# Causal mask of the first attention blocks: from GpSimd, after the exponential, to VectorE, before it

## The chip, the cores and the metric

The kernel runs on one core of a Trainium2 chip. The metric is the time on the device in microseconds (us) for one execution of the whole program. A profile of one execution gives, for each engine, when each instruction started, how long it was busy and what it waited for.

## What is computed

The reference is a small model of two layers on 2 x 2048 tokens of width 256. The first layer adds causal self-attention with 16 heads of width 16 and a feed-forward part with eight experts, of which a router picks two for each token; the second adds a state-space (Mamba) part and a ternary projection. The change lies in the attention, cut to what matters here:

```python
scores = jnp.einsum('bhqd,bhkd->bhqk', q, k) * scale
causal = jnp.tril(jnp.ones((s, s), dtype=bool))
scores = jnp.where(causal[None, None, :, :], scores, -jnp.inf)
weights = jax.nn.softmax(scores, axis=-1)
attn = jnp.einsum('bhqk,bhkd->bhqd', weights, v)
```

The router (`top_k` over eight logits) decides to which expert's rows each token is copied.

## The kernel before

The program is a chain of parts: layer norms and projections (to about 184 us), attention together with the router, the experts (from 1285 us), and the state-space part (from about 1925 us). Tile, the layer under the kernel, orders each engine's instructions when the program is built; on the chip every engine then runs its own list in that order and waits on semaphores.

Attention works on 16 stages, one for each pair of heads of each batch element (`stages()`). A stage has two passes over the causal half of the score matrix, in chunks of `CH` = 512 queries, `NJ` = 4 of them:

- `maxima(s)`: PE computes scores `m` of 128 queries by up to 512 keys for both heads (L652). On the diagonal block VectorE adds a mask (L662, 0 or a large negative number) in PSUM. VectorE then takes the row maxima into `best` (L665). When a chunk is done, its negated maxima are turned into rows, `tops` (L668 to L687).
- `attend(s)`: PE computes the scores transposed, 128 keys (`kb`) by 512 queries, into `s`, and adds the negated maxima with a second pair of matmuls (both L750). ScalarE (ACT) writes the exponential to `p` in SBUF (L758). Where the key block lies on the diagonal (`kb >= QT * j`, 4 of them in a chunk, 16 in a stage, 256 in all), GpSimd (POOL) sets the upper triangle of `p` to zero with an affine select (L763). PE multiplies `p` by the values (`values`, L705, tile `pv`).

The two passes run interleaved: in each tick a generator for `attend` and one for `maxima` advance by one block, `attend` 22 ticks (`LAG`) behind. Both passes draw their score tiles from one PSUM pool of three buffers (tag `sc`). The products of a block are issued one to two ticks after its exponential (`due`, `now`). The q and k of a stage are loaded on SyncE's queue (L554) from DRAM into a pool of three buffers, one stage ahead.

The router's work is spread between these ticks: every third step of the loop advances the generator `routing` by one. After some vector work in the first stages it loads 32 blocks of 128 rows on SyncE's queue (L973), and for each issues two indirect scatters on GpSimd (L984, tile `x_d`, 64 in all) that copy the rows to their experts' places. All scatters write the one DRAM tile `x_d`, so each waits for the one before. `routing` ends when the scatters are issued; the loop goes on with attention alone.

Of the kernel before, what the change touches and what calls it, by code (L numbers as in the profile page):

```python
# [11 lines left out]
F32 = mybir.dt.float32  # L12
F32R = mybir.dt.float32r
AF = mybir.ActivationFunctionType
ALU = mybir.AluOpType
# [4 lines left out]
P = 128  # L20
# [24 lines left out]
BIG = 3.0e38  # L45
# [56 lines left out]
def tile_model(ctx: ExitStack, tc: tile.TileContext, t, out):  # L102
# [55 lines left out]
    with ExitStack() as c0:  # L158
# [9 lines left out]
        with tc.tile_pool(name="vs", bufs=1) as vsp, tc.tile_pool(name="qk", bufs=3) as qk:  # L168
# [6 lines left out]
            with tc.tile_pool(name="pa", bufs=2) as pa, tc.tile_pool(  # L175
# [144 lines left out]

            routes = []
            attention(
                tc,
                t,
# [215 lines left out]
def stages():  # L540

    return [(b, pr) for b in range(B) for pr in range(H // 2)]
# [19 lines left out]
def attention(tc, t, ident, ones, qk, qk_d, stacks, v, xa, router):  # L562
# [6 lines left out]
    nc = tc.nc  # L569
    NJ = S // CH  # L570
    QT = CH // P
# [3 lines left out]
    with ExitStack() as ctx:  # L575
        w = ctx.enter_context(tc.tile_pool(name="at_w", bufs=1))
# [10 lines left out]
        for g in range(NG):  # L587
# [9 lines left out]
            out=mask,  # L597
            in_=mask,
            pattern=[[-1, P]],
            compare_op=ALU.is_ge,  # L600
            fill=-BIG / 10,
            base=0,
            channel_multiplier=1,
        )
        zeros = w.tile([P, P], BF, name="zeros")
        nc.gpsimd.memset(zeros, 0.0)

# [86 lines left out]
        def attend(s, attn):  # L694

            b, pr = stages()[s]
            qT, kT = stacks[s]

            def values(j, kb, off, pt):
                for h in range(2):  # L700
                    for f in range(2):
                        lo, hi = max(off, f * HC), (f + 1) * HC
                        if lo < hi:
                            r0 = 32 * (2 * h + f)
                            nc.tensor.matmul(  # L705
                                pv[r0 : r0 + HS + 1, lo - f * HC : HC],
                                lhsT=v[:, b * TPB + kb, 2 * pr + h, :],
                                rhs=pt[:, h, lo:hi],
                                start=(kb == 0),
                                stop=(kb == (QT * j + 1 if f == 0 else QT * j + 3)),  # L710
                                tile_position=(0, r0),
                            )

            def finish(j, raw):
                u = f"{s}_{j}"
                tr = ps_m.tile([P, 2, 2, 2, 32], F32, tag="misc", name=f"tr_{u}")
                for k in range(2):
                    nc.tensor.transpose(
                        tr[:, k].rearrange("p h f i -> p (h f i)"), raw[:, k * P : (k + 1) * P], ident
                    )  # L720
                inv = sm.tile([P, 2, 2, 2], F32, tag="inv", name=f"inv_{u}")
                nc.vector.reciprocal(inv, tr[:, :, :, :, HS])
                for f in range(2):
                    c0 = 2 * pr * HS
                    nc.vector.tensor_tensor(
                        attn[j][:, 2 * f : 2 * f + 2, c0 : c0 + 2 * HS].rearrange("p k (h i) -> p k h i", i=HS),
                        tr[:, :, :, f, 0:HS],
                        inv[:, :, :, f].unsqueeze(3).to_broadcast([P, 2, 2, HS]),
                        ALU.mult,
                    )  # L730
                if pr == H // 2 - 1:
                    done.append(output(b, j, attn[j]))

            def leave(j):
                raw = sm.tile([P, HC], F32, tag="raw", name=f"raw_{s}_{j}")
                nc.scalar.copy(raw, pv)
                turns.append(lambda: finish(j, raw))

            for j in range(NJ):
                if pr == 0:  # L740
                    attn[j] = vp.tile([P, QT, D], F32, tag="attn", bufs=4, name=f"attn_{b}_{j}")
                tp = tops.pop((s, j))
                for kb in range(QT * (j + 1)):
                    off = max(0, kb - QT * j) * P
                    ps = ps_s.tile([P, 2, CH], F32, tag="sc", name=f"s_{s}_{j}_{kb}")
                    pt = pp.tile([P, 2, CH], F32, tag="pt", name=f"p_{s}_{j}_{kb}")
                    for i in range(2):
                        for h in range(2):
                            hs = slice(HP * h, HP * (h + 1))
                            nc.tensor.matmul(  # L750
                                ps[:, h, off:CH],
                                lhsT=(kT[hs, kb * P : (kb + 1) * P], onesr[hs, :])[i],
                                rhs=(qT[hs, j * CH + off : (j + 1) * CH], tp[hs, off:CH])[i],
                                start=(i == 0),
                                stop=(i == 1),
                                tile_position=(HP * h, 0),
                            )
                    nc.scalar.activation(  # L758
                        pt[:, :, off:CH], ps[:, :, off:CH], AF.Exp, scale=float(HS) ** -0.5
                    )  # L760
                    if kb >= QT * j:
                        dg = pt[:, :, off : off + P]
                        nc.gpsimd.affine_select(  # L763
                            out=dg,
                            in_=dg,
                            pattern=[[0, 2], [1, P]],
                            compare_op=ALU.is_ge,
                            fill=0.0,
                            base=0,
                            channel_multiplier=-1,  # L770
                        )
                    due.append(lambda a=(j, kb, off, pt): values(*a))
                    if kb == QT * (j + 1) - 1:
                        due.append(lambda j=j: leave(j))
                    yield

        def output(b, j, attn):

            aT = sm.tile([P, 2, CH], F32, tag="aT", bufs=1, name=f"aT_{b}_{j}")
            for k in range(2):  # L780
                ps = ps_m.tile([P, CH], F32, tag="misc", name=f"aTp_{b}_{j}_{k}")
                for i in range(QT):
                    nc.tensor.transpose(
                        ps[:, i * P : (i + 1) * P], attn[:, i, k * P : (k + 1) * P], ident
                    )
                nc.scalar.copy(aT[:, k, :], ps)
                yield
            for c in range(2):
                po = ps_m.tile([P, 2, D], F32, tag="misc", name=f"po_{b}_{j}_{c}")
                for i in range(2):  # L790
                    at = (2 * c + i) * P
                    for k in range(2):
                        nc.tensor.matmul(
                            po[:, i, :],
                            lhsT=aT[:, k, at : at + P],
                            rhs=wo[:, k, :],
                            start=(k == 0),
                            stop=(k == 1),
                        )
                n0 = b * TPB + j * QT + 2 * c  # L800
                nc.vector.tensor_tensor(xa[:, n0 : n0 + 2, :], xa[:, n0 : n0 + 2, :], po, ALU.add)
                yield
# [10 lines left out]
        def second():  # L813
            for s in range(n_stages):
                yield from attend(s, attn)

        routing = router(rt, ps_m)
# [4 lines left out]
        for at, x in enumerate(tiles):  # L822
            if at % 3 == 0:
                now = due[:]
                del due[:]
                turn = turns.pop(0) if turns else None
            next(x, None)
            if at % 3 == 2:
                for f in now:
                    f()  # L830
                if turn:
                    turn()
                elif done and next(done[0], done) is done:
                    done.pop(0)
                next(routing, None)
        for x in (one, two):
            for _ in x:
                pass
# [1128 lines left out]
```

## Time and profile before

| | |
|---|---|
| median of 3 runs | 3077.14 us (3073.25 to 3079.84) |
| profiled execution, its own time | 3080.93 us |
| its span, first to last instruction | 3079.2 us |
| mean granted TensorE clock | 0.897 of full |
| PE busy | 2634.9 us (86%) |
| DVE (VectorE) busy | 2043.7 us (66%) |
| ACT (ScalarE) busy | 1592.4 us (52%) |
| POOL (GpSimd) busy | 1187.6 us (39%) |
| L763, the select on GpSimd | 256 times, 103.3 us busy |
| L984, the scatters on GpSimd | 64 times, median 972 ns each |

In the profile PE is the matrix engine and PEld its weight loads, DVE is VectorE, ACT ScalarE, POOL GpSimd, SP SyncE. A row of the waits reads: the engine and line that waited, the engine and line that it waited for, the sum in us, the number of waits and the longest. A row of the windows reads: the stretch, its length, and for each engine its busy time and number of instructions, then the clock that TensorE was granted as a share of full speed, and the share of time in which the DMA engines were busy. A row of the groups has the line, engine, operation, the tile written and read, the shapes and count; behind the bar stand the busy time in us, the mean of one in ns, and the idle time ahead of it with what ended that. A row of the timeline has the start, the duration, the instruction, and in brackets the idle time ahead of it.

### The profile page before, as it was taken

How to read it: one execution, taken by the hardware profiler on the slowest of the kernel's cores; microseconds unless marked ns; L12 is line 12 of the kernel's file. 1: busy time of each engine (PE TensorE's matmuls, PEld its weight loads, DVE VectorE, ACT ScalarE, POOL GpSimd, SP SyncE). 2: the span in 40 equal slices, each digit the busy share in tenths (PEclk: the TensorE clock that was granted, in tenths of full speed). 3: DMA queues.
4: the chain of work that ended last, by engine and by line, in shares of the span. 5: the costliest groups of instructions: out<-in, count | busy, mean ns of one | idle time of the engine just before them, and what ended most of it. 6: DMA issues, size and time to landing. Idle time of an engine off the chain costs nothing. (4 is left out here: it accounts for less than half of the span.)

```text
span 3079.2 us, 39986 instructions
## 1 busy us (share of the span) xinstructions
PE 2634.9 (86%) x15021; PEld 1493.3 (48%) x15021; DVE 2043.7 (66%) x2558; ACT 1592.4 (52%) x2546; POOL 1187.6 (39%) x934
## 2 busy tenths in 40 slices
PE   6887888999999999799999999577778888788747
PEld 4543433445444444488888888333333343333303
DVE  6576766888788888324111011258999999999996
ACT  3424555666566666422222222456766676666643
POOL 4313223010111011111111111247887978878775
PEclk9978988999999999899999999677887888879758
DMA  8843214112232220434345553323544535445350
GB/s 290 214 133 80 57 51 86 29 29 42 50 48 29 29 29 1 151 134 144 133 150 194 183 193 109 77 54 85 120 111 104 131 78 133 110 102 117 82 116 14
DMA packets 120614, 309.58 MB, mean 101 GB/s; under 512 B 28464, under 2 KB 70832, under 8 KB 102880
## 3 DMA queue, kind: packets, MB, share of 16 engines
q1 hardware_dynamic: 100496, 206.57, 28.3%
q0 software_dynamic: 18576, 99.24, 9.6%
q8 instruction: 122, 2.00, 0.3%
q10 hardware_dynamic: 1344, 1.16, 0.1%
q14 instruction: 76, 0.62, 0.1%
HBM read 228.51 MB, written 78.38 MB: 100 GB/s over the span
## 5 line engine op out<-in xcount | busy, mean ns | idle before, releaser
L758 ACT ACTIVATE p<-s 128x1024 f32<-128x1024 f32 (+3 forms) x640 | 563.2, 900 | 382.4 <-PE s L750 361.5
L665 DVE TENSOR_REDUCE best<-m 128x2 f32<-128x1024 f32 (+3 forms) x640 | 669.6, 1062 | 111.6 <-PE m L652 101.0
L1855 POOL TENSOR_TENSOR hh<-hh,cc 128x2048 f32<-128x2048 f32 x128 | 579.9, 4531 | 10.3
L1843 DVE TENSOR_TENSOR_SCAN hh<-decay,uh 128x2048 f32<-128x2048 f32 x128 | 565.9, 4421 | 23.8 <-ACT decay L1729 10.1
L705 PE MATMUL pv<-p,v 128*17 128x256 f32 (+1 forms) x4608 | 383.8, 379 | 49.0 <-POOL p L763 46.1
L763 POOL TENSOR_SCALAR_AFFINE_SELECT p<-p 128x256 f32<-128x256 f32 x256 | 103.3, 408 | 785.6 <-ACT p L758 784.5
L1729 ACT ACTIVATE decay<-dd,a_neg 128x511 f32<-128x511 f32 x512 | 332.9, 712 | 53.4 <-DVE hh L1843 52.8
L1118 ACT ACTIVATE hT<-h,b1s 128x256 f32<-128x256 f32 x296 | 137.7, 473 | 384.3 <-PE h L1111 384.3
L1132 DVE TENSOR_TENSOR yt<-o,b 128x512 f32<-128x512 f32 x37 | 25.6, 692 | 436.9 <-PE o L1124 436.9
L1753 DVE TENSOR_TENSOR uh<-dd,bb 128x2048 f32<-128x2048 f32 x128 | 293.6, 2294 | 21.5 <-PE bb L1740 11.6
L750 PE MATMUL s<-q,k 64*128 64x512 f32 (+3 forms) x1280 | 288.2, 437 | 22.9 <-DVE best L665 17.6
L652 PE MATMUL m<-k,q 64*128 64x512 f32 (+3 forms) x1280 | 281.6, 426 | 17.6 <-DVE best L665 8.9
L1111 PE MATMUL h<-xT,w 128*128 128x256 f32 x1184 | 276.1, 387 | 19.7 <-ACT hT L1118 8.1
L1124 PE MATMUL o<-w,hT 128*128 128x256 f32 x1184 | 262.7, 380 | 0.0
L1074 POOL DMA_INDIRECT w<-in_w,wrow x74 | 71.1, 961 | 479.2 <-PE h L1111 255.5
L1111 PEld LDWEIGHTS h<-xT,w 128*128 128x128 f32 x1184 | 226.7, 193 | 54.8 <-ACT hT L1118 8.5
L750 PE MATMUL s<-tops,onesr 64*128 64x512 f32 (+3 forms) x1280 | 248.5, 371 | 0.0
L1124 PEld LDWEIGHTS o<-w,hT 128*128 128x128 f32 x1184 | 225.7, 191 | 30.9
L1770 PE MATMUL y<-hh,sel 128*32 128x512 f32 x1024 | 162.1, 710 | 78.8 <-POOL hh L1855 78.6
L705 PEld LDWEIGHTS pv<-p,v 128*17 128x17 f32 x4608 | 107.9, 97 | 232.4 <-issue 113.5
L750 PEld LDWEIGHTS s<-q,k 64*128 64x128 f32 x1280 | 127.0, 188 | 168.1 <-DVE best L665 56.6
L652 PEld LDWEIGHTS m<-k,q 64*128 64x128 f32 x1280 | 129.3, 192 | 131.7 <-ACT p L758 68.1
(341 smaller groups left out, 3477.2 us busy)
## 6 DMA issues: line engine op xcount, KB each, us to landing
dd<-dd_d SPq DMA_DIRECT2D x120, 512.0 KB, 7.1
q<-qk_d SPq DMA_DIRECT2D x128, 128.0 KB, 5.1
k<-qk_d SPq DMA_DIRECT2D x128, 128.0 KB, 7.5
x_d<-zero SPq DMA_DIRECT2D x6, 1664.0 KB
xg<-x_d SPq DMA_DIRECT2D x37, 256.0 KB, 6.6
y_d<-yt SPq DMA_DIRECT2D x37, 256.0 KB
qk_d<-qp SPq DMA_DIRECT2D x16, 512.0 KB, 7.3
qk_d<-kp SPq DMA_DIRECT2D x16, 512.0 KB, 4.0
```

The source lines that it names most:

```text
L652: nc.tensor.matmul(ps[:, h, 0:n], lhsT=qT[hs, qs], rhs=kT[hs, c * CH : c * CH + n], start=True, stop=True, tile_position=(HP * h, 0),)
L665: nc.vector.tensor_reduce(best[:, i, :, c], ps[:, :, 0:n], AX.X, ALU.max)
L705: nc.tensor.matmul(pv[r0 : r0 + HS + 1, lo - f * HC : HC], lhsT=v[:, b * TPB + kb, 2 * pr + h, :], rhs=pt[:, h, lo:hi], start=(kb == 0), s ...
L750: nc.tensor.matmul(ps[:, h, off:CH], lhsT=(kT[hs, kb * P : (kb + 1) * P], onesr[hs, :])[i], rhs=(qT[hs, j * CH + off : (j + 1) * CH], tp[h ...
L758: nc.scalar.activation(pt[:, :, off:CH], ps[:, :, off:CH], AF.Exp, scale=float(HS) ** -0.5)
L1111: nc.tensor.matmul(ph, lhsT=w1[:, k * DF + f * P : k * DF + (f + 1) * P], rhs=xT[:, k, :], start=(k == 0), stop=(k == 1),)
L1124: nc.tensor.matmul(po[:, h, :], lhsT=hT[:, f, h * P : (h + 1) * P], rhs=w2[:, f * D : (f + 1) * D], start=(f == 0), stop=(f == NF - 1),)
L1729: nc.scalar.activation(decay[G % 2][:, q, 1:], of[at]["dd", n // 4][:, 0, q, 1:], AF.Exp, scale=a_neg[:, q, n : n + 1],)
L1753: nc.vector.tensor_tensor(uh, of[at]["dd", n // 4][:, 1], of[at]["bb", n].to_broadcast(full), ALU.mult)
L1770: nc.tensor.matmul(of[at]["y"][C4 * q : C4 * (q + 1), :], lhsT=sel, rhs=hh[:, q, :], start=False, stop=(g == 3), tile_position=(0, C4 * q),)
L1843: nc.vector.tensor_tensor_scan(hh.rearrange("p q c -> p (q c)"), decay[G % 2].rearrange("p q c -> p (q c)"), uh.rearrange("p q c -> p (q c)"),
L1855: nc.gpsimd.tensor_tensor(hh, hh, m_["cc", g].to_broadcast(full), ALU.mult)
```

## The change

A second mask, `mask_t`, is built once on GpSimd: 0 where the query is not before the key, a large negative number elsewhere. A list, `routed`, is empty until the generator `routing` has ended. While it is empty, the diagonal blocks of `attend` get `mask_t` added in PSUM by VectorE before the exponential, which makes the masked weights zero. From then on the select on GpSimd follows the exponential as before. In the program as built, the first 72 of the 256 diagonal blocks take the new way, and 184 the old.

```diff
+        mask_t = w.tile([P, P], F32, name="mask_t")
+        nc.gpsimd.memset(mask_t, 0.0)
+        nc.gpsimd.affine_select(
+            out=mask_t,
+            in_=mask_t,
+            pattern=[[1, P]],
+            compare_op=ALU.is_ge,
+            fill=-BIG / 10,
+            base=0,
+            channel_multiplier=-1,
+        )
+        routed = []
...
+                    if kb >= QT * j and not routed:
+                        dg = ps[:, :, off : off + P]
+                        nc.vector.tensor_tensor(
+                            dg, dg, mask_t.unsqueeze(1).to_broadcast([P, 2, P]), ALU.add
+                        )
                     nc.scalar.activation(
                         pt[:, :, off:CH], ps[:, :, off:CH], AF.Exp, scale=float(HS) ** -0.5
                     )
-                    if kb >= QT * j:
+                    if kb >= QT * j and routed:
                         dg = pt[:, :, off : off + P]
                         nc.gpsimd.affine_select(
...
-                next(routing, None)
+                if next(routing, routed) is routed:
+                    routed.append(True)
```

## The prediction

> **What bounds the kernel now.** I read the slices of the page first, to find the stretch that the change touches.
>
> ```profile
> PE   6887888999999999799999999577778888788747
> DVE  6576766888788888324111011258999999999996
> POOL 4313223010111011111111111247887978878775
> PEclk9978988999999999899999999677887888879758
> ```
>
> A slice is 77 us. Attention runs from 184 to 1285 us, slices 3 to 17. In its first five slices PE is at 7 or 8 tenths with a granted clock below full; after that it is at 9. The chain that ended last starts at 1944 us, in the state-space part, so it says nothing here, but attention ends before anything behind it starts, so what it loses the span loses. Next the windows. I cut attention where `attend` begins a new head pair (the first exponential, L758, of each group of 40), so that every row holds the same work: the matmul count, 538 to 546, shows it.
>
> ```profile
> core 0: us, PE busy (x) PEld busy (x) DVE busy (x) ACT busy (x) POOL busy (x), PEclk, DMA share, GB/s
> 209.90:289.70 79.80, 69.23 (x542) 32.18 (x544) 59.30 (x122) 40.79 (x61) 23.09 (x33) 0.85 0.16 49
> 289.70:360.80 71.10, 60.02 (x538) 28.55 (x536) 51.85 (x84) 40.08 (x60) 16.49 (x27) 0.90 0.26 54
> 360.80:437.30 76.50, 62.34 (x542) 28.46 (x538) 51.29 (x85) 40.14 (x61) 18.66 (x28) 0.91 0.27 59
> 437.30:510.80 73.50, 63.67 (x546) 29.59 (x544) 52.26 (x85) 39.93 (x60) 22.98 (x33) 0.91 0.33 78
> 510.80:584.20 73.40, 60.85 (x538) 28.78 (x538) 52.32 (x85) 40.09 (x61) 13.65 (x24) 0.88 0.25 47
> 584.20:646.30 62.10, 59.36 (x542) 27.54 (x538) 51.17 (x85) 39.98 (x61) 6.46 (x16) 1.00 0.24 34
> 646.30:707.00 60.70, 58.80 (x546) 28.12 (x544) 52.09 (x85) 39.75 (x60) 6.45 (x16) 1.00 0.26 38
> ```
>
> The first five stages take 79.8 + 71.1 + 76.5 + 73.5 + 73.4 = 374.3 us. Eight later ones, leaving out the two that also project the first batch element, take 59.5 to 62.2, mean 61.0, with PE busy 58.6, DVE 51.7 and ACT 39.9. Five such stages would be 305: the first five lose 69 us. PE itself splits the loss: it is idle 58.2 us in them against 12.1 in five later ones (46 more), and busy 316.1 against 292.8 (23 more, the same matmuls at a lower clock). Then who was waited for, from 209.9 to 584.2 us:
>
> ```profile
> POOL p L763 <- ACT p L758: 166.2, 41, 26.2
> POOL x_d L984 <- DMA x_d<-rows,slots: 127.0, 55, 7.9
> PEld pv L705 <- POOL p L763: 55.8, 29, 11.3
> PE pv L705 <- POOL p L763: 45.6, 15, 11.0
> ```
>
> PE waits 45.6 us, in 15 pieces, for masks on GpSimd, and that is the 46 of extra idle. GpSimd itself waits 127 us for its scatters to land. The timeline shows one case whole:
>
> ```profile
> 529.26 0.39 PE L750 MATMUL s<-q,k 64*128 64x256 f32 x2 [0.18 <-DVE best L665]
> ...
> 533.54 0.97 POOL L984 DMA_INDIRECT x_d<-rows,slots  x1 [7.66 <-DMA x_d<-rows,slots]
> 536.28 0.97 POOL L984 DMA_INDIRECT x_d<-rows,slots  x1 [1.77 <-DMA x_d<-rows,slots]
> 537.27 1.12 POOL L763 TENSOR_SCALAR_AFFINE_SELECT p<-p 128x256 f32<-128x256 f32 x3
> 537.74 0.15 PEld L705 LDWEIGHTS pv<-p,v 128*17 128x17 f32 x8 [8.18 <-POOL p L763]
> 537.74 1.06 PE L705 MATMUL pv<-p,v 128*17 128x256 f32 x8 [7.97 <-POOL p L763]
> ```
>
> A scatter waits until the one before it has landed, 2.7 us from issue to issue, and up to 8.6 when the load of the next q and k is in flight. Masks of 0.41 us stand behind it in GpSimd's order, and PE, whose order is fixed too, stops at the first product that needs one.
>
> **The change, part by part.** In the built order 72 masks (16 in each of the first four stages, 8 in the fifth) leave GpSimd and become an add on VectorE between the score matmuls and the exponential. On GpSimd all 64 scatters now stand ahead of the remaining 184 masks.
>
> *Setup.* One more memset and select on GpSimd: 0.29 + 0.29 us by the same pair at 183 us. GpSimd then rests until 211 us, so nothing; without that cover 0.6 us.
>
> *Removed.* Of the 69 us I leave 7.6 where they are: the first stage has DVE at 59.3 against 51.7, and this is the router's own vector work, which stays. The rest, 62 us, I give to the scatters, idle time and lowered clock alike: -62. The clock part is the less certain, and PE's 45.6 us of idle alone is the lower bound. The Trainium skill ("TensorE: Matmul & The Clock Gate", Part 1 and "HAM oscillation") has an idle window of about 3.4 us halve the clock and prices the lowered time at half of it. The windows give 1 - PEclk times length, summed over the five, as 41 us, so by that rule the loss would be 46 + 41 = 87 us where the rows give 69: part of the lowered time fell where PE was idle anyway, so the rows decide.
>
> *Added.* VectorE gets 72 adds of 128x256 f32 in PSUM plus a broadcast mask, which is exactly the form that L662 runs already:
>
> ```profile
> L665 DVE TENSOR_REDUCE best<-m 128x2 f32<-128x1024 f32 x114 | 137.5, 1221 | 15.5 <-PE m L652 14.0
> L662 DVE TENSOR_TENSOR m<-m,mask 128x256 f32<-128x256 f32 x64 | 27.5, 429 | 12.4 <-PE m L652 9.7 <-ACT p L758 2.0 <-issue 0.6
> ```
>
> 72 x 0.429 = 30.9 us, or 6.9 in a full stage. Does DVE's idle time cover it? A stage has 61.0 - 51.7 = 9.3 us of it, which would be enough, but not where the adds come. They come four in a row, one to a diagonal block, and in those runs (5.1 to 7.4 us long in the later stages) DVE has 0.1 to 1.3 us idle, about 0.6, and PE less. Perfect packing leaves 1.72 - 0.6 = 1.1 us of a run, 19 us for 18 runs. Nothing absorbs semaphore gaps, so I take the full price, 31 us.
>
> *The wait that is added.* VectorE's add waits for PE's score matmuls. Behind it on VectorE stand the next row-maximum reductions; the exponential waits for it on ACT, and PE waits for that exponential, because the next `m` tile takes the buffer that it frees (three are shared). How long an add sits behind a reduction the trace of before cannot show. From below: the hop through GpSimd between exponential and product goes, worth 8.2 us in 28 waits from 560 to 1200 us, 0.05 us a mask, -3.5 us in all. From above: every add waits out a whole 1.22 us reduction, 72 x 1.22 = 88 us. In the built order the add stands nearly always ahead of the reduction of the same tick, as PE produces them; 8 of 72 stand ahead of a reduction whose tile PE finishes first. I take zero, nearest the row of L662, which waited 12.4 us in 64 cases for its matmuls, DVE being early rather than late.
>
> *Queues.* Scatters no longer stand behind masks. The row loads on SyncE wait for scatters as before, and the q and k loads behind them have more than a stage of lead. SyncE also holds back rows until a q buffer is free, once a stage. So the last row comes as the fifth stage starts, and its two scatters end some 12 us later (two of 2.7 and one slow landing); the first mask left on GpSimd is the fifth stage's ninth, about 30 us in. Nothing is added; if it fails, one stall like those of before, 8 to 11 us.
>
> *Sum.* -62 + 31 = -31 us. By stage: 61 + 7.6 + 6.9 = 75.5, three of 67.9, one of 64.4: 343.6 against 374.3. The profiled execution took 3080.9 us (span 3079.2), 3.8 above the median of 3077.1; -31 gives 3050 for it and 3046 for the median.
>
> **Rivals.**
>
> *Slack hides the adds.* DVE's 9.3 us a stage is taken up after all, PE running ahead by its buffers. For: 6.9 is below 9.3. Against: the runs above have no such room. Cost 0 to 15 us, time 3015 to 3030, say 3022 (cost 7).
>
> *VectorE's queue becomes the bound, and it is slower.* On average an add finds a reduction half done: 0.43 + 0.61 = 1.04 us on the path for each mask, 75 us, so 62 saved and 75 paid: +13, 3090. It decides from 62 / 72 = 0.86 us a mask. For: DVE would be at 58.6 of 61.0 us, 96%, and exponential, buffer and next matmul form a loop through it. Against: PE feeds both in DVE's order. The Trainium skill ("Perfetto Trace Analysis", Optimizing Scalar/DVE Operations) says to move work off a saturated DVE, to GPSIMD if need be, the opposite of this edit; the 85% that DVE shows in the later stages says that it isn't saturated yet.
>
> *The scatters still reach the path.* Unhindered they run into the fifth stage, or the slow clock stays for another reason: idle comes back by one or two stalls and half of the 16 us of clock (62 - 46): 3046 + 18 = 3064.
>
> **How the numbers follow.** The forecast has 0.60 (cost 19 to 45 us, so 3034 to 3060), slack 0.13, queue 0.13, scatters 0.14. A measurement of this kernel can tell about 0.2%, 6 us. Slower by that is the queue case, with a little of it that only breaks even: 0.12. Within 6 us: 0.06, from its edge and the worst of the scatter case. Faster: 0.82. The range goes from slack at its likely price, 3022, to 3072, where the last of the gain is still there; left out are most of the queue case and the bottom of the slack case.
>
> **What would show it.** Right: a VectorE row of 72 adds near 429 ns; L763 at 184; PE's wait for GpSimd at L705 under 5 us from 45.6; PEclk 1.00 from the second stage on; stages of 64 to 68 us with DVE at 58 to 59; scatters 2.7 us apart, without masks between. Wrong: the stages stay over 72 with PE now waiting for ACT at L652 or for DVE at L750 (queue), fall to 62 (slack), or GpSimd's first mask comes right behind a scatter with PE waiting (scatters). If the clock stays below 1.00 without stalls, my giving all 16 us of it to the scatters was wrong.

## The result and the profile after

The changed kernel takes 3027.8 us (median of 4 runs, 3027.2 to 3030.9) against 3075.2 us for the kernel before beside it (3073.1 to 3079.8): a ratio of 0.985, 95% interval 0.983 to 0.986, or 47 us less. The forecast was 31 us less, 3046, with a range from 3022 to 3072. The direction, the place and the removed stall came as forecast; the price of the added work was put at about twice what it is. The profiled execution took 3027.2 us, with a span of 3025.5.

The slices of the page of the changed kernel (76 us each; attention is in slices 3 to 17):

```profile
PE   6879999999999999799999997677878788887846
DVE  6569888887888886232110101368999999999996
POOL 4302221110001101111112111268897887978875
PEclk9969999999999999899999998787887878889758
```

PE is at 9 tenths from the fourth slice on, where before it stayed at 7 and 8 through the seventh. Then the windows of the changed kernel, cut by the same rule, at the first exponential of a head pair:

```profile
core 0: us, PE busy (x) PEld busy (x) DVE busy (x) ACT busy (x) POOL busy (x), PEclk, DMA share, GB/s
210.80:283.30 72.50, 67.77 (x546) 30.79 (x544) 62.59 (x136) 41.37 (x62) 14.00 (x14) 0.89 0.11 35
283.30:346.60 63.30, 59.50 (x544) 27.94 (x540) 56.54 (x101) 40.10 (x62) 15.45 (x16) 1.00 0.41 91
346.60:412.30 65.70, 61.24 (x544) 27.50 (x540) 56.30 (x101) 40.52 (x61) 13.52 (x14) 1.00 0.38 77
412.30:477.70 65.40, 61.45 (x544) 28.36 (x540) 56.60 (x101) 40.30 (x61) 17.38 (x18) 1.00 0.39 87
477.70:537.90 60.20, 56.55 (x532) 27.00 (x530) 52.98 (x91) 39.49 (x60) 5.18 (x10) 1.00 0.25 38
```

The five stages sum to 327.1 us, 47.2 less than the 374.3 of before. The clock is full from the second on, and the later stages agree with those of before within 0.4 us (62.2 against 62.1, 61.0 against 60.7 and so on). So the whole gain lies in these five. (In the two profiled executions the span differs by 53.7; of that 8.1 us lie behind attention, where the work is the same. In the profiles below, that part took between 1796 and 1806 us; I therefore compare stages rather than spans wherever a few us matter.)

The waits of the changed kernel, 210.8 to 537.9 us:

```profile
POOL x_d L1003 <- DMA x_d<-rows,slots: 135.7, 59, 8.1
ACT p L776 <- DVE s L773: 57.9, 55, 7.0
PEld m L665 <- ACT p L776: 41.4, 83, 1.2
PEld pv L718 <- POOL p L781: 0.4, 1, 0.4
```

The lines have moved: L1003 is the scatter, L773 the new add, L776 the exponential, L781 the select, L718 the product with the values. GpSimd waits for its scatters as long as ever, but nothing waits for it any more. PE's wait for GpSimd has gone from 55.8 us in 29 waits (the weight loads of `pv`) to 0.4 in one, and no wait of PE's own matmuls on it is left. A smaller one has come: the exponential now waits for VectorE, 57.9 us in 55 waits, and PE's load for the next `m` waits for the exponential twice as often (41.4 us in 83 waits; 20.0 in 49 before).

VectorE's groups, 283.3 to 537.9 us, hold the new row:

```profile
L675 DVE TENSOR_TENSOR m<-m,mask 128x256 f32<-128x256 f32 x64 | 27.4, 429 | 9.7 <-PE m L665 8.0 <-issue 0.4 <-ACT tops L700 0.4
L773 DVE TENSOR_TENSOR s<-s,mask_t 128x256 f32<-128x256 f32 x55 | 23.3, 424 | 1.6 <-PE s L763 0.9 <-PE m L665 0.6
```

### The profile page after: what moved, and what is told of

The parts are those of the page before. It is cut to its first block, busy times and chain, and to the rows that moved or that the text cites. A ratio compares the mean times of both kernels' runs of the same rounds, so it can differ in the third digit from the quotient of the medians.

```text
span 3025.5 us, 39961 instructions
## 1 busy us (share of the span) xinstructions
PE 2616.7 (86%) x15021; PEld 1484.5 (49%) x15021; DVE 2063.7 (68%) x2630; ACT 1592.7 (53%) x2546; POOL 1159.4 (38%) x864
## 5 line engine op out<-in xcount | busy, mean ns | idle before, releaser
L776 ACT ACTIVATE p<-s 128x1024 f32<-128x1024 f32 (+3 forms) x640 | 564.3, 900 | 337.9 <-PE s L763 256.3
L678 DVE TENSOR_REDUCE best<-m 128x2 f32<-128x1024 f32 (+3 forms) x640 | 670.7, 1063 | 68.4 <-PE m L665 58.6
L718 PE MATMUL pv<-p,v 128*17 128x256 f32 (+1 forms) x4608 | 377.6, 373 | 4.3 <-ACT raw L749 3.8
L781 POOL TENSOR_SCALAR_AFFINE_SELECT p<-p 128x256 f32<-128x256 f32 x184 | 74.4, 406 | 664.6 <-ACT p L776 663.9
L1789 PE MATMUL y<-hh,sel 128*32 128x512 f32 x1024 | 163.7, 716 | 76.8 <-POOL hh L1874 76.6
L718 PEld LDWEIGHTS pv<-p,v 128*17 128x17 f32 x4608 | 106.8, 96 | 181.5 <-issue 114.0
```

The source lines that it names most:

```text
L678: nc.vector.tensor_reduce(best[:, i, :, c], ps[:, :, 0:n], AX.X, ALU.max)
L718: nc.tensor.matmul(pv[r0 : r0 + HS + 1, lo - f * HC : HC], lhsT=v[:, b * TPB + kb, 2 * pr + h, :], rhs=pt[:, h, lo:hi], start=(kb == 0), s ...
L776: nc.scalar.activation(pt[:, :, off:CH], ps[:, :, off:CH], AF.Exp, scale=float(HS) ** -0.5)
L1789: nc.tensor.matmul(of[at]["y"][C4 * q : C4 * (q + 1), :], lhsT=sel, rhs=hh[:, q, :], start=False, stop=(g == 3), tile_position=(0, C4 * q),)
```

## The experiments

Three questions were open: is the stall that went wholly the scatters' doing, what do the adds cost by themselves, and why. Stages in us, cut as above, first to fifth:

| kernel | 1 | 2 | 3 | 4 | 5 | sum |
|---|---|---|---|---|---|---|
| before | 79.8 | 71.1 | 76.5 | 73.5 | 73.4 | 374.3 |
| changed | 72.5 | 63.3 | 65.7 | 65.4 | 60.2 | 327.1 |
| before, no scatters | 68.8 | 59.5 | 62.2 | 60.6 | 59.6 | 310.7 |
| changed, no scatters | 72.8 | 63.1 | 65.8 | 65.4 | 60.3 | 327.2 |
| changed, product after the exponential | 66.6 | 61.4 | 63.9 | 61.8 | 60.7 | 314.4 |
| changed, each add twice | 76.8 | 74.6 | 74.8 | 72.6 | 65.4 | 364.2 |
| changed, again | 69.0 | 63.1 | 65.8 | 65.4 | 60.3 | 323.6 |

### The kernel before without its scatters

```diff
-            nc.gpsimd.indirect_dma_start(
-                out=x_d[:, :],
-                out_offset=bass.IndirectOffsetOnAxis(ap=slots[:, i, n : n + 1], axis=0),
-                in_=rows,
-                in_offset=None,
-            )
```

> The kernel before, with the 64 scatters left out (the experts then work on empty rows; the masks stay on GpSimd). Theory A, masks stand behind scatters on GpSimd and PE waits for them: the five slow stages go to 61 us, the first to about 69 with the router's vector work, so 62 us less than before, 3013, and PE's wait for GpSimd at the value products falls from 45.6 us to under 2. Rival B, the slow clock and the idle time have another cause (the router's vector work, the loads of q and k): the stages stay over 70 and the time within 15 us of before.

Measured: 3012.9 us (3010.9 to 3014.1), ratio to before 0.979 (0.978 to 0.981), 61.5 us less than the 3074.4 beside it. Its windows:

```profile
210.80:279.60 68.80, 64.76 (x540) 30.23 (x540) 59.00 (x122) 40.61 (x62) 6.75 (x16) 0.92 0.21 59
279.60:339.10 59.50, 56.83 (x538) 27.31 (x538) 51.84 (x85) 39.86 (x60) 6.50 (x16) 1.00 0.25 35
339.10:401.30 62.20, 59.48 (x542) 27.62 (x538) 51.30 (x85) 40.06 (x61) 6.45 (x16) 1.00 0.27 36
401.30:461.90 60.60, 58.70 (x546) 28.15 (x544) 51.99 (x85) 39.84 (x60) 6.50 (x16) 1.00 0.27 37
461.90:521.50 59.60, 56.92 (x538) 27.23 (x538) 51.90 (x85) 39.87 (x60) 6.50 (x16) 1.00 0.26 36
```

With the router's vector work (DVE 59.0 in the first stage) and the q and k loads still there and the scatters gone, stages two to five are undisturbed ones and the clock is full in them. Rival B falls: idle time and lowered clock were both the scatters'. One thing more moves in this run: with no scatter to wait for, the 32 row loads on SyncE are all issued by 262.5 us, where before they ran until 519.6. They aren't the cause, since in the changed kernel they run until 475.2 without a stall. PE's own wait for GpSimd at the products, 45.6 us before, is gone, as expected (under 2); the weight loads' wait there is down from 55.8 us to 4.0 in 14 waits of at most 0.4, the ordinary hop from select to product.

The first stage keeps 7.8 us over 61.0, but its row says something else than the prediction did. PE is busy 64.8 us in it, against 58.6 in an undisturbed stage, and idle only 1.6 us more. The granted clock is 0.50 in the stage's first 10.8 us and full after them, 0.92 over the whole stage. PE is busy for 10.0 us of these 10.8, so as an estimate the half clock is worth up to 5 of the 7.8 us. Most of it, then, is a low clock at the start of attention, and not PE waiting for the router's vector work; no run here leaves that work out.

### The changed kernel without its scatters

The same lines are taken out of the changed kernel.

> The changed kernel, with the 64 scatters left out (the experts work on empty rows). Theory A, the scatters are wholly off the path once no mask stands behind them: the same as the changed kernel, 3028, and about 15 us above the kernel before without scatters, which is the price of the 72 adds (0.2 us each, not the 0.43 that I took). Rival D, the scatters still cost something beside the masks (traffic, row loads in front of the q and k loads): well below, 3013 to 3020, and the adds cost nearly nothing.

Measured: 3023.8 us (3023.1 to 3035.9), ratio 0.983 (0.981 to 0.985). The median lies 2 to 4 us under the two medians of the changed kernel, less than the part behind attention varies, so the stages decide: 327.2 against 327.1, and each of the five within 0.3 us. Rival D falls. Once no mask stands behind them, the scatters cost nothing, whether by their traffic or by the row loads on SyncE, which here too are all issued early (by 265.3 us). And the 72 adds cost 327.1 - 310.7 = 16.4 us, 0.23 each. Stages two to five alone, with 56 adds, give 254.6 - 241.9 = 12.7, again 0.23. By the medians the price comes out at 11 to 15 us; so 16 is its upper end.

### All 256 masks added by VectorE

```diff
-                    if kb >= QT * j and not routed:
+                    if kb >= QT * j:
...
-                    if kb >= QT * j and routed:
+                    if False:
```

> The changed kernel with all 256 masks added by VectorE, none left on GpSimd. It measures the price of 16 adds in a stage where nothing else is going on. By the stages of the changed kernel (2 to 5 us a stage over 61, say 4): 11.5 more stages, 46 us, 3074. By the price on record, 6.9 us a stage: 79 us, 3107. If the adds are free and the extra of the changed kernel's stages comes from the scatters: 3028.

Measured: 3067.4 us (10 runs, 3064.1 to 3072.5), ratio 0.998 (0.997 to 0.999): nearly all of the gain is spent. Against the kernel without scatters, four undisturbed stages (the eleventh to the fourteenth) take 63.1, 65.5, 65.7 and 63.4 us where that has 59.6, 62.1, 60.7 and 59.7: 3.9 us for 16 adds, 0.24 each. So the price is the same with the router and without it. My 3074 was 7 us too high, and 3107, by the price of the prediction, 40.

### The mask after the exponential

```diff
-                    if kb >= QT * j and not routed:
-                        dg = ps[:, :, off : off + P]
-                        nc.vector.tensor_tensor(
-                            dg, dg, mask_t.unsqueeze(1).to_broadcast([P, 2, P]), ALU.add
-                        )
                     nc.scalar.activation(
                         pt[:, :, off:CH], ps[:, :, off:CH], AF.Exp, scale=float(HS) ** -0.5
                     )
+                    if kb >= QT * j and not routed:
+                        dg = pt[:, :, off : off + P]
+                        nc.vector.tensor_tensor(
+                            dg, dg, mask_t.unsqueeze(1).to_broadcast([P, 2, P]), ALU.mult
+                        )
```

`mask_t` then holds 1 and 0.

> The changed kernel with the first 72 masks still on VectorE, but as a product with a 0/1 mask in SBUF after the exponential, so that the exponential and the PSUM buffer no longer wait for VectorE. If what the adds cost is VectorE's time: 3028 again, with a few us for a shorter or longer instruction. If it is the later exponential and with it the later release of the PSUM buffer: most of the 15 us goes, 3014 to 3018, and PE's wait at L665 for ACT falls back.

Measured: 3012.6 us (3010.8 to 3013.3), ratio 0.980 (0.978 to 0.981): as fast as with no scatters at all, and faster than both kernels. The product is as long as the add (median 416 ns against 423) and VectorE as busy (55.8 us in the second stage against 56.5), but PE's load for `m` waits for the exponential only 17.8 us in 45 waits, down from 41.4 in 83:

```profile
PEld m L665 <- ACT p L771: 17.8, 45, 0.9
```

This speaks for the second reading: the add's cost came mostly from its place. The run changes two things at once, though: the product stands behind the exponential, and it works in SBUF and no longer in PSUM.

### Each add twice

```diff
-                        nc.vector.tensor_tensor(
-                            dg, dg, mask_t.unsqueeze(1).to_broadcast([P, 2, P]), ALU.add
-                        )
+                        for _ in range(2):
+                            nc.vector.tensor_tensor(
+                                dg, dg, mask_t.unsqueeze(1).to_broadcast([P, 2, P]), ALU.add
+                            )
```

> The changed kernel with each of the 72 adds done twice (72 more of 0.42 us on VectorE, all ahead of their exponentials). If the low price of the first add (16 us for 72, 0.23 each) comes from idle time of VectorE that it fills, the second finds less of it and costs nearer to its full 0.42: 26 to 31 us, 3054 to 3059. If the price is only a fixed delay of waiting in VectorE's queue, paid once, the second adds its own length less than wholly: 10 to 16 us, 3038 to 3044.

Measured: 3070.1 us (9 runs, 3063.9 to 3075.9), ratio 0.997 (0.996 to 0.999). The second add costs 364.2 - 327.1 = 37 us, 0.52 each (41 us against the second profile of the changed kernel): more than either reading gave, and more than its length. It isn't that VectorE had no idle time left:

```profile
292.00:366.60 74.60, 65.89 (x541) 29.72 (x539) 62.32 (x117) 40.24 (x60) 19.45 (x20) 0.89 0.39 91
366.60:441.40 74.80, 67.03 (x544) 29.42 (x542) 62.36 (x117) 40.62 (x61) 12.64 (x13) 0.91 0.32 62
```

VectorE rests 12 us in each of these, and the clock has fallen again, so the first reading, that the second add finds no idle time to fill, falls as well. The timeline of this kernel shows what happens:

```profile
306.70 1.22 DVE L678 TENSOR_REDUCE best<-m 128x2 f32<-128x1024 f32 x1
307.83 0.42 DVE L774 TENSOR_TENSOR s<-s,mask_t 128x256 f32<-128x256 f32 x1
308.17 1.22 DVE L678 TENSOR_REDUCE best<-m 128x2 f32<-128x1024 f32 x1
309.30 0.75 DVE L774 TENSOR_TENSOR s<-s,mask_t 128x256 f32<-128x256 f32 x2
```

The scheduler set a 1.22 us reduction between the two adds of one block, and the exponential stands behind all of it (L774 is the add here); taking VectorE's adds in pairs, such a reduction stands in 35 of the 72. So this run lengthened the delay and not only the work, and it doesn't price an add by itself. Nor are its 37 us all delay: PE is idle 20 us longer than in the changed kernel and busy 17 us longer, with a clock of 0.89 to 0.95. How much each part is worth this run doesn't separate.

### All masks after the exponential

The kernel with the product, with the two conditions changed as for all 256 adds.

> All 256 masks as a product on VectorE in SBUF after the exponential, none on GpSimd. Beside the run with all 256 adds ahead of the exponential (3067) it prices the same work at the other place. Theory C, the add costs mostly because exponential and buffer release wait for it: the products cost the 0.7 us a stage that they cost in the first five stages, 3013 + 8 = 3021. If VectorE's time is what counts: the same 4 us a stage as the adds, 3067 less the router's stages, some 3055.

Measured: 3029.1 us (3027.4 to 3034.0), ratio 0.984 (0.983 to 0.986), where the same masks ahead of the exponential gave 3067. The four stages compared above take 61.4, 63.9, 61.7 and 61.7 us: 1.65 us over the kernel without scatters, against 3.9 for the adds. The 8 us that I expected rested on 0.7 us a stage, a mean over five that the first stage had spoiled: in it the product kernel was 2.2 us faster than the one without scatters, and in the next three it was 1.2 to 1.9 us slower, 1.6 in the mean, which agrees with the 1.65. PE's waits for the exponential, four stages each; ahead of it (all 256 adds, 878.2 to 1135.8 us), then behind it (all 256 products, 853.8 to 1102.5 us):

```profile
PEld m L665 <- ACT p L776: 37.2, 72, 1.2
PE m L665 <- ACT p L776: 9.8, 25, 0.8
```

```profile
PEld m L665 <- ACT p L771: 15.7, 39, 0.9
PE m L665 <- ACT p L771: 1.2, 5, 0.4
```

With the select on GpSimd the first of these rows has 18.9 us in 47 waits in four undisturbed stages of the changed kernel.

### The changed kernel again

> The changed kernel once more, beside the others on this chip: 3028, the first five stages at 327 us, and the part behind attention, whose instructions are the same in all these kernels, anywhere from 1796 to 1806 us, as in the profiles so far.

Measured: 3025.5 us (3023.7 to 3028.7), ratio 0.983 (0.982 to 0.985). Stages two to five agree with the first profile within 0.2 us. The first stage took 69.0 us, not 72.5: in this execution the half clock that stands at the start of attention in every kernel lasted 34.1 us and reached 5.4 us into the stage, in the other 44.4 us and 15.8. So the first stage, and with it a sum of five, moves by 3.5 us from one execution to another without any change of the kernel.

## Why the prediction was right, and where not

**Removed: 62 us.** Right, nearly to the us: 61.5 by time, 63.6 by stages. The 7.6 us left in the first stage are there too, 68.8 against 61.0, but their reason was a different one: mostly the half clock at the start of attention, which before lasted as long as in the kernel without scatters (37.5 us each), and not the router's vector work. That the size agrees with VectorE's 7.6 us is at least in part luck. The split between idle time and clock needn't be known for the 62. The rule of the Trainium skill ("TensorE: Matmul & The Clock Gate", Part 1) that idle windows lower the clock agrees with the rows: 0.85 to 0.91 with the stalls, 1.00 from the second stage on without them. Its price for the lowered time, half of it, would have given 87 us, 79 without the first stage's 7.6; the rows gave 62, and 61.5 to 63.6 came. A long idle window isn't needed for a low clock, though: with each add done twice it fell to 0.89 to 0.95 in the second to fourth stage, where PE's matmuls waited at most 1.1 us at a time. What lowered it there stays open.

**Added: 31 us. This is the step that failed**, as written: "Nothing absorbs semaphore gaps, so I take the full price, 31 us." The adds cost 16.4. The 0.429 us of the row was taken as time on VectorE, and all of that time as time on the path. Neither holds.

Of the first: the timeline shows that neighbours overlap. In the run above an add starts at 307.83, before the reduction of 1.22 us from 306.70 has ended, and the next reduction starts at 308.17, before the add has; from start to start the add takes 0.34 us. Busy time counts what overlaps only once, and over the five stages VectorE is busy 285.0 us with the adds and 266.0 in the kernel without scatters and adds: 19.0 us for 72, or 0.26 each (0.28 in the four undisturbed stages with 16 adds each). The Trainium skill ("Perfetto Trace Analysis", Optimizing Scalar/DVE Operations) says as much: the reported latency is about twice the busy time of the fixed overhead, since the write acknowledgement overlaps with the next instruction. That the overlap in this trace is that acknowledgement is not shown here; the size, 0.42 us reported and 0.26 to 0.28 used, is.

Of the second: behind the exponential the same masks make VectorE busy 16.0 us longer in four stages, but the stages only 6.6 us longer. So idle time does take up much of the work. (The sum in the prediction for perfect packing is slightly off, too: 1.1 us in each of 18 runs is 20 us, not 19.)

**The added wait.** I took zero for it. The runs with the product show that it isn't: 16 masks on VectorE cost 3.9 us ahead of the exponential and 1.65 behind it, with VectorE busy 18.1 and 16.0 us more in four stages. More than half of the adds' price, 2.2 us of 3.9, goes with the place ahead of the exponential, and PE's shorter waits for the exponential point to the buffer that PE gets later. These runs can't wholly tell the place from the product's working in SBUF; but VectorE's busy time differs by 2.1 us in the four stages, and the stages differ by 8.9.

So two terms were off in opposite directions. Scaled from 16 masks to 72, an estimate, VectorE's work alone cost about 7 us where I had 31, and the wait about 10 where I had nothing. That the 31 came within a factor of two of the 16.4 is in part luck.

**Setup and queues.** The setup can't be seen: attention's first exponential comes at 208.4 to 215.2 us in the profiles of the changed kernel and its variants, and at 209.9 before. The queues went as forecast. The last scatter starts at 488.3 us, 10.6 after the fifth stage began (forecast: done 12 us in), and the first mask on GpSimd at 509.7, 32 in (forecast 30), so nothing waits:

```profile
488.33 0.97 POOL L1003 DMA_INDIRECT x_d<-rows,slots  x1 [7.57 <-DMA x_d<-rows,slots]
509.67 0.40 POOL L781 TENSOR_SCALAR_AFFINE_SELECT p<-p 128x256 f32<-128x256 f32 x1 [20.37 <-ACT p L776]
```

**The stages.** Forecast 75.5, three of 67.9 and 64.4; measured 72.5, 63.3, 65.7, 65.4 and 60.2: each 2 to 5 us lower, as the adds cost less. VectorE is busy 56.3 to 56.6 us in the second to fourth, where the prediction asked for 58 to 59.

**The rivals.** The forecast's own case, 3034 to 3060, did not come: the measured 3027.8 lies in the range of *Slack hides the adds* (3015 to 3030), which had a chance of 0.13. Its mechanism, VectorE's idle time taken up, is there behind the exponential (6.6 of 16.0 us reach the path); ahead of it the added wait took most of that back, so that the rival isn't what happened either. *VectorE's queue becomes the bound* did not come with one add of 0.23 us on the path, but the doubled add, at 0.74 a mask in all ((364.2 - 310.7) / 72), comes close to its limit of 0.86 and to the time of before, in part by the lowered clock. *The scatters still reach the path* is excluded by the two runs without them.

## What to carry over

Short work that the busiest engine waits for doesn't belong in the in-order queue of an engine that issues transfers which wait for each other: 0.41 us masks cost 62 us there, though that engine was idle most of the time. When moving it, look not only at the time of the new engine but at where on the chain it stands: behind the instruction that frees the shared buffer, nearly the same work cost less than half. And for an engine's time take the growth of its busy time (0.26 to 0.28 us an add here), or the distance from start to start (0.34), not the duration in the row (0.42).

## What was not expected of the hardware

An add of 0.42 us by its row took 0.34 us from start to start in a filled queue, and 0.26 to 0.28 us of VectorE's busy time on average. And a second add of 0.42 us ahead of 72 exponentials, with the reduction that came to stand between, was enough to bring the lowered clock back (0.89 to 0.95 in the middle stages of the doubled add), without any wait of an exponential above 3.8 us, or of PE's matmuls above 1.1 us, in these stages.
